# Another layout for the state recurrence of a Mamba block: 16 states x 8 channels on the partitions

## The chip, the core and the metric

The kernel runs on one core of a Trainium2 chip. The metric is the device time of one execution in microseconds; all times below are microseconds unless marked ns. The engines are called PE (matrix engine; PEld its weight loads), DVE (vector engine), ACT (scalar engine), POOL (GpSimd) and SP, whose queue issues the DMAs.

## The reference

Input `x` has 64 channels, 256 steps of t and 128 of f. Layer 0 runs a two-way Mamba block along t and then along f; layer 1 is a windowed two-way convolutional LSTM. The change concerns the recurrence of layer 0, which runs for each of four parameter sets (two passes, two directions):

```python
xz = einsum('nld,ed->nle', rmsnorm(u), in_proj_w); x, z = split(xz, 2)   # 128 channels each
x  = silu(conv1d_depthwise(x, 4 taps) + conv_b)
dt, Bm, Cm = split(x @ x_proj_w.T, [4, 20])                              # 4, 16 and 16 wide
dt = softplus(dt @ dt_proj_w.T + dt_proj_b)                              # 128 channels
A  = -exp(A_log)                                                         # (128, 16)
def step(h, inp):                                                        # h: (n, 128, 16)
    dA = exp(dt_t[:, :, None] * A)
    h = dA * h + dt_t[:, :, None] * B_t[:, None, :] * x_t[:, :, None]
    return (h, einsum('nds,ns->nd', h, C_t))
y = (ys + x * Dp) * silu(z); out = y @ out_proj_w.T + u
```

So for each token there are 128 channels x 16 states: a decay, an input, a recurrence along the sequence, a product with C, and a sum over the states.

## The kernel before, in words

Layer 0 works in two passes, the class `Stage`: along t (stage 0, sequences of 256 tokens) and along f (stage 1, sequences of 128). A chunk is 512 tokens of whole sequences; each pass has 64 chunks. `run` issues, for every chunk: `scan` of direction 0, then `head` of the next chunk (both directions), `scan` of direction 1, and `tail`. The program is written in a framework whose scheduler places each engine's instructions in a fixed order when the program is built and adds the semaphores. A tile pool has a number of buffers for each tag; a new tile waits until the oldest one of its tag is free.

`head` loads `u` (by SP along t, by a POOL copy from `X` along f), normalises it (`sq`, `pm`, `rs`, `unp`), and takes both directions up to the scan's inputs: `px` and `pz` on PE, `xs` and `zs` (Silu) on ACT, `pv` on PE; then softplus over ACT (`e`, `r`, `lw`) and POOL (`w`, `e`, `lw`, `dt`), and `dtx` = dt * x on POOL. B and C (32 rows, `pb`) are split into three bfloat16 parts, stacked in the tile `bc` (L287 to L290), so that a bfloat16 matmul can spread one row over all partitions exactly.

In `scan` the 128 channels lie on the partitions, and the 512 tokens on the free axis. A round g treats two of the 16 states, side by side in 1024 columns; here it is called a pair, and a direction has eight. A pair is, with its lines:

- PE, L315: four bfloat16 matmuls spread B's and C's rows of the two states into PSUM, `bb` and `cc`, one buffer each.
- ACT, L321: two exponentials, dA = exp(A * dt), into one of two fixed buffers per direction.
- DVE, L325: bx = bb * dtx; L327: the scan h = dA * h + bx along 1024 columns; L335: h = h * cc.
- PE, L308: two float32 matmuls with the identity add the states of the pair before to `y`.

At the end of a direction L339 forms `yz` = y * silu(z). `tail` (L348 to L370) multiplies by the output weights, adds the residuals `u`, and ACT puts the result into `X`. A float32 matmul shows as two passes in the profile. Layer 1 follows (lines from L389 on) and is not touched; of its lines, the prediction names L466 (additions of weights on DVE and POOL), L458 (loads of those weights), L577 (matmuls over half of the rows), L605, L612 and L613 (DVE steps on `n` and `v`), and L616 (stores of `y` to `out`).

Of the kernel before, what the change touches and what calls it, by code (L numbers as in the profile page):

```python
"""TF-Mamba block followed by the windowed bidirectional conv-LSTM, on one core.

Layer 0 keeps channels (d = 128) on the partitions and tokens on the free axis.  A chunk is 512
tokens of whole sequences; its two directions share the normalised input.  Products of weights
alone are formed once on the chip: the depthwise taps with in_proj, dt_proj with x_proj, out_proj
with the closing linear layer.  The state recurrence is a scan along the free axis, run backwards
for the flipped direction; a zero decay at a sequence's first token starts it anew.

Layer 1 keeps (parity of f, channel) on the partitions, so that the stride 2 of the windows is a
step of one column.  Taps of the window and of the conv that meet the same column are summed once;  # L10
the four columns at the borders, where the conv's padding drops taps, have their own weights.
"""
# [18 lines left out]
P = 128  # L31
# [4 lines left out]
NBC = 2 * NS  # L36
RANK = 4
# [14 lines left out]
class Mamba:  # L52
    """What the chip keeps of the four parameter sets and the two closing linear layers."""

    def __init__(self, ctx, tc, d):
# [7 lines left out]
        # sel[32 k + s, s, :] = 1 for k = 0, 2, 3: spreads row s of a 32-row block over all  # L63
        # partitions and adds the three blocks.
        self.sel = cp.tile([P, NBC, P], BF16, name="sel")
        nc.vector.memset(self.sel, 0.0)
        for k in (0, 2, 3):
            rows = slice(NBC * k, NBC * (k + 1))
            nc.vector.tensor_copy(
                self.sel[rows],  # L70
                self.ident[rows, rows].unsqueeze(2).to_broadcast([NBC, NBC, P]),
            )

# [20 lines left out]
        # A = -exp(A_log)  # L94
        nc.scalar.preload_act_table_set(EXP_AND_LN)
        self.A = cp.tile([P, 4, NS], F32, name="A")
# [4 lines left out]
        self.G1, self.G2, self.Wz, self.Wdt, self.Wbc, self.Dd, self.W2 = ([] for _ in range(7))  # L101
        self.W3, self.lin_b = [], []
        with tc.tile_pool(name="m_prep", bufs=2) as pp, tc.tile_pool(
# [3 lines left out]
            for i, n in enumerate(("tlin", "flin")):  # L107
# [6 lines left out]
                # Both blocks' residuals and the layer's own: u @ (I + W_f + W_b).  # L114
# [7 lines left out]
            for i in range(4):  # L122
# [17 lines left out]
                # Rows 64-127 of the moving operand lag one token behind rows 0-63.  # L140
# [13 lines left out]
                # B and C, three times; nothing in rows 32-63.  # L154
                wbc = cp.tile([P, 4, NBC], F32, name=f"wbc{i}", tag=f"wbc{i}")
                nc.vector.memset(wbc, 0.0)
                for k in (0, 2, 3):
                    nc.vector.tensor_copy(wbc[:, k], xbc)
                self.Wbc.append(wbc.rearrange("p k s -> p (k s)"))
# [12 lines left out]
class Stage:  # L172
    """One bidirectional pass over all tokens, chunk after chunk: along t, or along f."""

    def __init__(self, ctx, m, stage, L, X):
# [6 lines left out]
        self.io = ctx.enter_context(tc.tile_pool(name=n + "io", bufs=2))  # L182
        self.wk = ctx.enter_context(tc.tile_pool(name=n + "wk", bufs=2))
        self.st = ctx.enter_context(tc.tile_pool(name=n + "st", bufs=2))
        fixed = ctx.enter_context(tc.tile_pool(name=n + "fixed", bufs=1))
        self.ps_mm = ctx.enter_context(tc.tile_pool(name=n + "mm", bufs=3, space=PSUM))
        self.ps_bc = ctx.enter_context(tc.tile_pool(name=n + "bc", bufs=1, space=PSUM))
        self.ps_y = ctx.enter_context(tc.tile_pool(name=n + "y", bufs=1, space=PSUM))

        # The padding columns of unp and the decays that start a sequence stay zero throughout.  # L190
# [17 lines left out]
    def head(self, ch, src):  # L208
        """Loads chunk ch, normalises it, and takes both directions up to the scan's inputs."""
        nc, m, L, nseq = self.nc, self.m, self.L, self.nseq  # L210
        unp = self.unp[ch % 2]
        if self.time:
            u = self.io.tile([C, nseq, L], F32, name="u", tag="u", bufs=3)
            nc.sync.dma_start(out=u, in_=src[:, ch * nseq : (ch + 1) * nseq, :])
            blocks = [(slice(0, C), slice(0, nseq), u, m.ones_lo[0:C])]
        else:
            u = self.io.tile([P, nseq // 2, L], F32, name="u", tag="u", bufs=3)
            rows = slice(ch * nseq // 2, (ch + 1) * nseq // 2)
            nc.gpsimd.tensor_copy(u, self.X[:, rows, :])  # L219
            blocks = [  # L220
                (slice(0, C), slice(0, nseq // 2), u, m.ones_lo),
                (slice(C, P), slice(nseq // 2, nseq), u, m.ones_hi),
            ]

        sq = self.io.tile(list(u.shape), F32, name="sq", tag="sq")
        nc.gpsimd.tensor_mul(sq, u, u)  # L226
# [3 lines left out]
        # (mean + eps) ** -0.5  # L230
# [8 lines left out]
        for d in range(2):  # L239
# [5 lines left out]
            xs = self.wk.tile([P, NTOK], F32, name="xs", tag=f"xs{d}")  # L245
# [3 lines left out]
            zs = self.wk.tile([P, NTOK], F32, name="zs", tag=f"zs{d}")  # L249
# [3 lines left out]
        # One table set serves all functions from here to the next chunk's Silu.  # L253
        with self.tc.issue_after(silu.ins):
            preload = nc.scalar.preload_act_table_set(EXP_AND_LN)
        for d in range(2):
            i = 2 * self.stage + d
            xs, zs = out[d]
            # softplus(v) = max(v, 0) + log(1 + e), e = exp(-|v|); w = fl(1 + e) and
            # log(1 + e) = log(w) + (e - (w - 1)).  # L260
# [3 lines left out]
            r = self.wk.tile([P, NTOK], F32, name="r", tag="r", bufs=1)  # L264
            lw = self.wk.tile([P, NTOK], F32, name="lw", tag="lw", bufs=1)
            w1 = self.wk.tile([P, NTOK], F32, name="w1", tag="w1", bufs=1)
            with self.tc.issue_after(preload.ins):
                nc.scalar.activation(e, pv, AF.Abs, bias=m.dtb[:, i : i + 1])
            nc.scalar.activation(r, pv, AF.Relu, bias=m.dtb[:, i : i + 1])
            nc.scalar.activation(e, e, AF.Exp, scale=-1.0)  # L270
            nc.scalar.activation(lw, e, AF.Ln, bias=1.0)  # L271
            nc.gpsimd.tensor_scalar(w1, e, 1.0, -1.0, ALU.add, ALU.add)  # L272
            nc.gpsimd.tensor_sub(e, e, w1)  # L273
            nc.gpsimd.tensor_add(lw, lw, e)  # L274
            dt = self.wk.tile([P, NTOK], F32, name="dt", tag=f"dt{d}")
            nc.gpsimd.tensor_add(dt, lw, r)  # L276
            dtx = self.wk.tile([P, NTOK], F32, name="dtx", tag=f"dtx{d}")
            nc.gpsimd.tensor_mul(dtx, dt, xs)  # L278
            # B and C without loss as a sum of three bfloat16: rows 0-31 hold the leading 8 bits of
            # the 24, rows 64-95 the next, rows 96-127 the rest. One pass of the tensor engine then  # L280
            # spreads a row over all partitions, and its float32 sum is the float32 it came from.
            lo, mid = slice(3 * NBC, P), slice(2 * NBC, P)
            pb = self.ps_mm.tile([P, NTOK], F32, name="pb", tag="mm")
            nc.tensor.matmul(pb, lhsT=m.Wbc[i], rhs=xs, start=True, stop=True)
            bc = self.wk.tile([P, NTOK], BF16, name="bc", tag=f"bc{d}")
            rest = self.wk.tile([P, NTOK], F32, name="rest", tag="rest", bufs=1)
            nc.scalar.copy(bc, pb)  # L287
            nc.vector.tensor_sub(rest[mid], pb[mid], bc[mid])  # L288
            nc.gpsimd.tensor_copy(bc[mid], rest[mid])
            nc.gpsimd.tensor_sub(bc[lo], rest[lo], bc[lo])  # L290
            out[d] = (xs, zs, dt, dtx, bc)
        return u, out

    def scan(self, d, ins):
        """The state recurrence of one direction and its gated output."""
        nc, m, L = self.nc, self.m, self.L
        i = 2 * self.stage + d
        xs, zs, dt, dtx, bc = ins
        y = self.ps_y.tile([P, NTOK], F32, name="y", tag="y")
        nc.tensor.matmul(y, lhsT=m.Dd[i], rhs=xs, start=True, stop=False)  # L300
        step = slice(None) if d == 0 else slice(None, None, -1)
        live = slice(1, L) if d == 0 else slice(0, L - 1)
        pending = None

        def add_up(g, h):
            for j in range(2):
                last = g == NS // 2 - 1 and j == 1
                nc.tensor.matmul(y, lhsT=m.ident, rhs=h[:, j], start=False, stop=last)  # L308

        for g in range(NS // 2):  # L310
            bb = self.ps_bc.tile([P, 2, NTOK], F32, name="bb", tag="bb")
            cc = self.ps_bc.tile([P, 2, NTOK], F32, name="cc", tag="cc")
            for k, to in ((0, bb), (NS, cc)):
                for j in range(2):
                    nc.tensor.matmul(to[:, j], lhsT=m.sel[:, k + 2 * g + j], rhs=bc, start=True, stop=True)  # L315
            if pending is not None:
                add_up(*pending)
            dA = self.dA[d][g % 2]
            for j in range(2):
                s = 2 * g + j  # L320
                nc.scalar.activation(  # L321
                    dA[:, j, :, live], self.seqs(dt)[:, :, live], AF.Exp, scale=m.A[:, i, s : s + 1]
                )
            bx = self.st.tile([P, 2, NTOK], F32, name="bx", tag="bx")
            nc.vector.tensor_mul(bx, bb, dtx.unsqueeze(1).to_broadcast([P, 2, NTOK]))  # L325
            h = self.st.tile([P, 2, NTOK], F32, name="h", tag="h", bufs=3)
# [8 lines left out]
            nc.vector.tensor_mul(h, h, cc)  # L335
            pending = (g, h)
# [5 lines left out]
    def tail(self, ch, u, yz):  # L342
        """Closing linear layer with the residuals; the result goes to its place in X."""
# [33 lines left out]
    def run(self, src):  # L377
        nch = T * F // NTOK
        u, ins = self.head(0, src)
        for ch in range(nch):  # L380
            yz = [self.scan(0, ins[0])]
            # The next chunk's head fills the gaps of this one's recurrence.
# [4 lines left out]


def group_norm(tc, X, xn, d):  # L389
    """xn = (X - mean) / sqrt(var + eps) * g + b over everything."""  # L390
    nc = tc.nc
    N = float(C * T * F)
    per = T * F * C // P
# [309 lines left out]
```

## Time and profile before

| what | value |
|---|---|
| median of 3 runs (lowest, highest) | 12018.28 (12006.94, 12019.82) |
| span of the profiled execution, first to last instruction | 12017.3 |
| mean granted PE clock | 0.946 |
| pass along t, 60 to 5365 | 5305, 82.9 a chunk |
| pass along f, 5365 to 10833 | 5468, 85.4 a chunk |
| layer 1, 10833 to 12017 | 1184 |
| L327, L335, L325 on DVE, 2048 each, mean | 2345 ns, 1211 ns, 1205 ns |
| L321 on ACT, 4096, mean | 712 ns |
| ACT table loads in layer 0, each | 1283 ns |
| bytes moved by DMA in the whole span | 28.01 MB |

The page gives the profiled execution's span; its time outside that span is not listed, and the span lies within the three runs. A group's line reads: line, engine, operation, written tile <- read tiles, shapes, count | busy time in total, mean ns of one | idle time of the engine before them, and what ended most of it. In an order of time the columns are start, duration, engine, line, operation, tiles, count.

### The profile page before, as it was taken

What the parts mean: (1) busy time and instruction counts of PE and PEld (TensorE: products, weight loads), DVE (VectorE), ACT (ScalarE), POOL (GpSimd) and SP (SyncE); (2) the same over time, 40 slices, a digit from 0 to 9 for tenths busy, and PEclk for the clock granted to TensorE, in tenths of its full rate; (3) what the DMA queues carried; (4) which work ended last, traced back from release to release, by engine and by line L of the source; (5) the groups of instructions that cost most, each with busy time, mean ns of one, the idle gap of its engine ahead of it and who ended that gap; (6) DMA issues with size and microseconds to landing.
All of it is one profiled execution on the core that took longest, in us unless ns stands there. A gap on an engine that the chain in (4) does not pass through costs nothing. (4 is left out here: it accounts for less than half of the span.)

```text
span 12017.3 us, 70162 instructions
## 1 busy us (share of the span) xinstructions
PE 9284.9 (77%) x24028; PEld 3706.5 (31%) x24028; DVE 10185.2 (85%) x7361; ACT 4977.8 (41%) x7263; POOL 3404.9 (28%) x2079
## 2 busy tenths in 40 slices
PE   6777777777777777777777777777777777777999
PEld 2222222222222222222222322223222222223554
DVE  8999999999999999988999999989999999992121
ACT  4444444444444444434444444444444444431111
POOL 3223232232232322323223323233333233221111
PEclk9999999999999999989999999999999999998999
DMA  0000000000000000000000000000000000000000
GB/s 6 2 2 2 2 2 2 2 2 2 2 2 2 2 2 2 2 1 0 0 0 0 0 0 0 0 0 0 0 0 0 0 0 0 0 0 22 8 8 10
DMA packets 15447, 28.01 MB, mean 2 GB/s; under 512 B 4561, under 2 KB 5233, under 8 KB 15089
## 3 DMA queue, kind: packets, MB, share of 16 engines
q1 hardware_dynamic: 15088, 23.53, 0.6%
q8 instruction: 188, 3.08, 0.1%
q14 instruction: 171, 1.39, 0.0%
HBM read 15.14 MB, written 8.39 MB: 2 GB/s over the span
## 5 line engine op out<-in xcount | busy, mean ns | idle before, releaser
L327 DVE TENSOR_TENSOR_SCAN h<-dA,bx 128x1024 f32<-128x1024 f32 x2048 | 4803.2, 2345 | 48.1 <-ACT dA L321 2.0
L321 ACT ACTIVATE dA<-dt,A 128x510 f32<-128x510 f32 (+1 forms) x4096 | 2716.0, 712 | 4846.6 <-DVE h L327 4702.5
L308 PE MATMUL y<-h,ident 128*128 128x512 f32 x8192 | 4186.0, 636 | 197.5 <-DVE h L335 195.1
L335 DVE TENSOR_TENSOR h<-h,cc 128x1024 f32<-128x1024 f32 x2048 | 2479.2, 1211 | 201.1 <-PE cc L315 151.3
L325 DVE TENSOR_TENSOR bx<-bb,dtx 128x1024 f32<-128x1024 f32 x2048 | 2467.2, 1205 | 140.3 <-PE bb L315 131.5
L315 PE MATMUL bb<-bc,sel 128*128 128x512 bf16 x4096 | 1287.6, 396 | 1299.0 <-DVE bx L325 1288.0
L315 PEld LDWEIGHTS <-sel 128*128 128x128 bf16 x8192 | 793.7, 100 | 4618.3 <-issue 4238.6
L308 PEld LDWEIGHTS y<-h,ident 128*128 128x128 f32 x8192 | 1642.9, 203 | 1774.7 <-issue 1139.3
L315 PE MATMUL cc<-bc,sel 128*128 128x512 bf16 x4096 | 1291.7, 398 | 904.3 <-DVE h L335 891.3
L272 POOL TENSOR_SCALAR w<-e 128x512 f32<-128x512 f32 x256 | 596.6, 2331 | 3083.7 <-ACT e L270 3078.0
L553 PE MATMUL pg<-xn,acc 128*128 128x456 f32 x2048 | 815.9, 550 | 0.7 <-ACT gxe L480 0.7
L226 POOL TENSOR_TENSOR sq<-u 64x512 f32<-64x512 f32 (+1 forms) x128 | 179.5, 1403 | 1993.2 <-DMA u<-in_x 1986.3
L612 DVE TENSOR_SCALAR n<-v,slope 128x512 f32<-128x512 f32 x64 | 31.1, 487 | 775.9 <-ACT v L610 774.8
L219 POOL COPY u<-X 128x256 f32<-128x256 f32 x64 | 46.4, 725 | 2144.7 <-PE po L360 2144.6
L276 POOL TENSOR_TENSOR dt<-lw,r 128x512 f32<-128x512 f32 x256 | 515.2, 2013 | 20.1
L553 PEld LDWEIGHTS pg<-xn,acc 128*128 128x128 f32 x2048 | 375.5, 188 | 372.1 <-issue 348.8
L290 POOL TENSOR_TENSOR bc<-rest,bc 32x512 bf16<-32x512 f32 x256 | 452.5, 1767 | 20.4
L288 DVE TENSOR_TENSOR rest<-pb,bc 64x512 f32<-64x512 f32 x256 | 177.7, 694 | 329.5 <-POOL bc L290 177.2
L274 POOL TENSOR_TENSOR lw<-lw,e 128x512 f32<-128x512 f32 x256 | 440.4, 1720 | 20.2
L273 POOL TENSOR_TENSOR e<-e,w 128x512 f32<-128x512 f32 x256 | 402.0, 1570 | 26.2 <-ACT lw L271 6.6
L610 ACT ACTIVATE v<-pproj,bpr 128x512 f32<-128x512 f32 x32 | 22.0, 687 | 774.2 <-PE pproj L605 774.2
L278 POOL TENSOR_TENSOR dtx<-dt,xs 128x512 f32<-128x512 f32 x256 | 335.7, 1311 | 20.2
(129 smaller groups left out, 6911.3 us busy)
## 6 DMA issues: line engine op xcount, KB each, us to landing
u<-in_x SPq DMA_DIRECT2D x64, 128.0 KB, 2.5
out<-y SPq DMA_DIRECT2D x32, 256.0 KB, 2.0
w<-in_W_ih_f SPq DMA_DIRECT2D x5, 512.0 KB, 5.8
w<-in_W_ih_b SPq DMA_DIRECT2D x5, 512.0 KB
cw<-in_conv_w SPq DMA_DIRECT2D x4, 128.0 KB, 3.2
win<-in_in_proj SPq DMA_DIRECT2D x4, 64.0 KB, 2.2
wpr<-in_W_proj SPq DMA_DIRECT2D x1, 256.0 KB, 2.9
ow<-in_out_proj SPq DMA_DIRECT2D x4, 32.0 KB, 1.9
```

What stands on the lines that cost most here:

```text
L272: nc.gpsimd.tensor_scalar(w1, e, 1.0, -1.0, ALU.add, ALU.add)
L273: nc.gpsimd.tensor_sub(e, e, w1)
L274: nc.gpsimd.tensor_add(lw, lw, e)
L276: nc.gpsimd.tensor_add(dt, lw, r)
L290: nc.gpsimd.tensor_sub(bc[lo], rest[lo], bc[lo])
L308: nc.tensor.matmul(y, lhsT=m.ident, rhs=h[:, j], start=False, stop=last)
L315: nc.tensor.matmul(to[:, j], lhsT=m.sel[:, k + 2 * g + j], rhs=bc, start=True, stop=True)
L321: nc.scalar.activation(dA[:, j, :, live], self.seqs(dt)[:, :, live], AF.Exp, scale=m.A[:, i, s : s + 1])
L325: nc.vector.tensor_mul(bx, bb, dtx.unsqueeze(1).to_broadcast([P, 2, NTOK]))
L327: nc.vector.tensor_tensor_scan(h.rearrange("p j n -> p (j n)")[:, step], dA.rearrange("p j n l -> p (j n l)")[:, step], bx.rearrange("p j ...
L335: nc.vector.tensor_mul(h, h, cc)
L553: nc.tensor.matmul(pg[:, :, 2 : 2 + inner], lhsT=acc[:, q, gate * P : (gate + 1) * P], rhs=xv[:, rows, half, q : q + inner], start=q == 0, ...
```

## The change

The tile of the recurrence is turned: the partitions now hold 16 states x 8 channels (partition 8 s + d), and a group is 8 of the 128 channels; there are 16 groups, numbered 4 r + k. A pair is now two groups, (r, k) and (r + 1, k), again 1024 columns.

- `dt` has to be on all 16 states' partitions. It is written to a DRAM tile `there` (256 KB) and read back four times with a repeated source into the tiles `rep` (1 MB each, four buffers of one tag shared by both directions).
- `dtx` is spread by float32 matmuls whose contracted rows are 32 of the partitions (`sel`), into `bx` in PSUM (two buffers). DVE multiplies `bx` by B in place, and the scan reads it from PSUM.
- B and C come out of one float32 matmul each, already repeated over the 8 channels (`Wb`, `Wc`), and are copied to SBUF by ACT; the bfloat16 split is gone.
- The product with C moves from DVE to POOL.
- The sum over the states is a float32 matmul with 32 output columns (`fold`) into 32 of y's partitions, two per pair, in place of the identity matmuls. The input product and the fold are called spread and fold below.
- `sq` moves from POOL to ACT; w = 1 + e and w - 1 move to ACT as two Identity steps, `lw` is Ln of w.
- Pools: `io` 2 -> 1 buffers (`u` 3 -> 2), `wk` 2 -> 3 with tags shared by the directions, `st` 2 -> 3 (so `h` has three, as before).

```diff
+        mask = cp.tile([P, NK, DL], F32, name="mask")
...
+        self.sel = cp.tile([P, NK, P], F32, name="sel")
+        for k in range(NK):
             nc.vector.tensor_copy(
+                self.sel[:, k].rearrange("p (s d) -> p s d", s=NS),
+                mask[:, k].unsqueeze(1).to_broadcast([P, NS, DL]),
             )
+        self.fold = cp.tile([P, NK, 32], F32, name="fold")
...
-        self.io = ctx.enter_context(tc.tile_pool(name=n + "io", bufs=2))
-        self.wk = ctx.enter_context(tc.tile_pool(name=n + "wk", bufs=2))
-        self.st = ctx.enter_context(tc.tile_pool(name=n + "st", bufs=2))
+        self.io = ctx.enter_context(tc.tile_pool(name=n + "io", bufs=1))
+        self.wk = ctx.enter_context(tc.tile_pool(name=n + "wk", bufs=3))
+        self.st = ctx.enter_context(tc.tile_pool(name=n + "st", bufs=3))
+        self.dram = ctx.enter_context(tc.tile_pool(name=n + "dram", bufs=3, space=bass.MemoryType.DRAM))
...
-        self.ps_bc = ctx.enter_context(tc.tile_pool(name=n + "bc", bufs=1, space=PSUM))
+        self.ps_bx = ctx.enter_context(tc.tile_pool(name=n + "bx", bufs=2, space=PSUM))
...
-        nc.gpsimd.tensor_mul(sq, u, u)
+        nc.scalar.activation(sq, u, AF.Square)
...
-            nc.scalar.activation(lw, e, AF.Ln, bias=1.0)
-            nc.gpsimd.tensor_scalar(w1, e, 1.0, -1.0, ALU.add, ALU.add)
-            nc.gpsimd.tensor_sub(e, e, w1)
+            nc.scalar.activation(w, e, AF.Identity, bias=1.0)
+            nc.scalar.activation(lw, w, AF.Ln)
+            nc.scalar.activation(w, w, AF.Identity, bias=-1.0)
+            nc.gpsimd.tensor_sub(e, e, w)
             nc.gpsimd.tensor_add(lw, lw, e)
+            nc.gpsimd.tensor_add(dt, lw, dt)
+            there = self.dram.tile([DL, NG, NTOK], F32, name="there", tag="there")
+            nc.sync.dma_start(out=there.rearrange("d g t -> g d t"), in_=dt)
+            rep = []
+            for r in range(4):
+                t = self.wk.tile([P, NK, NTOK], F32, name="rep", tag="rep", bufs=4)
+                nc.sync.dma_start(
+                    out=t,
+                    in_=there[:, NK * r : NK * (r + 1)].unsqueeze(0).to_broadcast([NS, DL, NK, NTOK]),
+                )
+                rep.append(t)
...
-            nc.scalar.copy(bc, pb)
-            nc.vector.tensor_sub(rest[mid], pb[mid], bc[mid])
-            nc.gpsimd.tensor_copy(bc[mid], rest[mid])
-            nc.gpsimd.tensor_sub(bc[lo], rest[lo], bc[lo])
+            for h, wt in ((0, m.Wb[i]), (1, m.Wc[i])):
+                pb = self.ps_mm.tile([P, NTOK], F32, name="pb", tag="mm")
+                nc.tensor.matmul(pb, lhsT=wt, rhs=xs, start=True, stop=True)
+                t = self.wk.tile([P, NTOK], F32, name="bc", tag=f"bc{h}")
+                nc.scalar.copy(t, pb)
...
+        pairs = [[(r, k), (r + 1, k)] for r in (0, 2) for k in range(NK)]
+        def add_up(n, h):
+            for j, (r, k) in enumerate(pairs[n]):
+                nc.tensor.matmul(
+                    y[32 * r : 32 * r + 32],
+                    lhsT=m.fold[:, k],
+                    rhs=h[:, j],
...
+        for n, pair in enumerate(pairs):
+            bx = self.ps_bx.tile([P, 2, NTOK], F32, name="bx", tag="bx")
+            for j, (r, k) in enumerate(pair):
+                rows = slice(32 * r, 32 * r + 32)
+                nc.tensor.matmul(bx[:, j], lhsT=m.sel[rows, k], rhs=dtx[rows], start=True, stop=True)
             if pending is not None:
                 add_up(*pending)
+            dA = self.dA[d][n % 2]
+            for j, (r, k) in enumerate(pair):
+                g = NK * r + k
                 nc.scalar.activation(
+                    dA[:, j, :, live], self.seqs(rep[r][:, k])[:, :, live], AF.Exp, scale=m.A[:, i, g : g + 1]
                 )
-            bx = self.st.tile([P, 2, NTOK], F32, name="bx", tag="bx")
-            nc.vector.tensor_mul(bx, bb, dtx.unsqueeze(1).to_broadcast([P, 2, NTOK]))
-            h = self.st.tile([P, 2, NTOK], F32, name="h", tag="h", bufs=3)
+            nc.vector.tensor_mul(bx, bx, B.unsqueeze(1).to_broadcast([P, 2, NTOK]))
+            h = self.st.tile([P, 2, NTOK], F32, name="h", tag="h")
             nc.vector.tensor_tensor_scan(
...
-            nc.vector.tensor_mul(h, h, cc)
-            pending = (g, h)
+            nc.gpsimd.tensor_mul(h, h, Cm.unsqueeze(1).to_broadcast([P, 2, NTOK]))
+            pending = (n, h)
```

## The prediction

> **What bounds the kernel now.** I read four views: the engines' totals with the stretches by pass, the groups, the order of time within one chunk, and the few rows that stand for what the change adds. Times are microseconds; a "pair" is one round of the scan loop (two of 16 states), a chunk has 16 pairs, eight per direction.
>
> First the totals, then busy time in the pass along t and the pass along f (columns: stretch, its length, busy time of PE, weight loads, DVE, ACT, POOL, granted clock):
>
> ```profile
> PE 9284.9 (77%) x24028; PEld 3706.5 (31%) x24028; DVE 10185.2 (85%) x7361; ACT 4977.8 (41%) x7263; POOL 3404.9 (28%) x2079
> ...
> 60.00:5365.00 5305.00, 4035.71 (x10206) 1524.72 (x10204) 4895.25 (x3450) 2317.94 (x3432) 1461.39 (x949) 0.95 0.01 2
> 5365.00:10833.00 5468.00, 4109.69 (x10493) 1613.95 (x10493) 5027.21 (x3586) 2486.48 (x3576) 1794.42 (x1030) 0.93 0.00 0
> ```
>
> DVE is busy 92% of both passes. With 64 chunks each, a chunk takes 82.9 along t and 85.4 along f, 84.2 on average. The other 1244 of the span 12017.3 hold start-up and the second layer, which the change leaves alone. The groups say what fills DVE:
>
> ```profile
> L327 DVE TENSOR_TENSOR_SCAN h<-dA,bx 128x1024 f32<-128x1024 f32 x2048 | 4803.2, 2345 | 48.1 <-ACT dA L321 2.0
> L335 DVE TENSOR_TENSOR h<-h,cc 128x1024 f32<-128x1024 f32 x2048 | 2479.2, 1211 | 201.1 <-PE cc L315 151.3
> L325 DVE TENSOR_TENSOR bx<-bb,dtx 128x1024 f32<-128x1024 f32 x2048 | 2467.2, 1205 | 140.3 <-PE bb L315 131.5
> ```
>
> One steady pair in order of time (start, duration):
>
> ```profile
> 5012.26 1.19 DVE L325 TENSOR_TENSOR bx<-bb,dtx 128x1024 f32<-128x1024 f32 x1
> 5013.38 1.20 DVE L335 TENSOR_TENSOR h<-h,cc 128x1024 f32<-128x1024 f32 x1
> 5014.51 2.28 DVE L327 TENSOR_TENSOR_SCAN h<-dA,bx 128x1024 f32<-128x1024 f32 x1
> 5015.06 1.88 PE L308 MATMUL y<-h,ident 128*128 128x512 f32 x4
> 5016.71 1.19 DVE L325 TENSOR_TENSOR bx<-bb,dtx 128x1024 f32<-128x1024 f32 x1
> ```
>
> A pair takes 4.45, back to back on DVE. A float32 matmul of 512 columns is two passes, 0.43 apart: (1.88 - 0.59) / 3.
>
> **Rows for what is added.** POOL beside DVE, POOL's cost of a 1024-wide two-operand step, matmuls on half of the rows, and transfers:
>
> ```profile
> 5004.82 2.28 DVE L327 TENSOR_TENSOR_SCAN h<-dA,bx 128x1024 f32<-128x1024 f32 x1
> 5005.02 3.15 POOL L276 TENSOR_TENSOR dt<-lw,r 128x512 f32<-128x512 f32 x1
> 5007.02 1.20 DVE L325 TENSOR_TENSOR bx<-bb,dtx 128x1024 f32<-128x1024 f32 x1
> 5008.93 1.27 POOL L278 TENSOR_TENSOR dtx<-dt,xs 128x512 f32<-128x512 f32 x1
> ```
> ```profile
> L466 POOL TENSOR_TENSOR hi<-hi,w 128x1024 f32<-128x1024 f32 x8 | 19.7, 2464 | 25.2 <-issue 17.3 <-DMA w<-in_W_ih_f 7.5
> ```
> ```profile
> 11615.19 1.93 PE L577 MATMUL pg<-hs,whh 64*128 64x488 f32 x8
> ```
> ```profile
> out<-y SPq DMA_DIRECT2D x32, 256.0 KB, 2.0
> w<-in_W_ih_f SPq DMA_DIRECT2D x5, 512.0 KB, 5.8
> ```
>
> **DVE, removed.** The C product (16 x 1.21 a chunk), `rest` (2 x 0.69), and the fights of scan and POOL. The third group shows these: L276 stood still while the scan (both operands in SBUF) ran to 5007.05, then finished in 1.1 beside L325, whose one operand is in PSUM. After the change bx is in PSUM, so scan and product each read one operand from SBUF; I price no fights. The Trainium skill ("SBUF — State Buffer", "Who interferes with whom") says the same and extends it to any DVE step with one SBUF input; the scan with one operand in PSUM is in no row here. What remains: product, then a scan that needs it at once. L613 follows L612, which it needs, 0.03 after its end, so 1.20 + 0.03 + 2.28 = 3.5 a pair. Reading and writing bx in PSUM lies between nothing and the 0.02 by which the L325 and L335 rows differ from their minima; I take nothing. Floor of a chunk: 16 x 3.5 = 56.0, two `yz` (0.67), `unp` (2 x 0.67 along t, 4 x 0.42 along f): 58.7 and 59.0.
>
> **POOL.** It loses `w`, two `bc` steps and `sq`, and gains the C product, 2.36 (the uncontended L466; mean 2.46). Per chunk 16 x 2.36 = 37.8 plus eight 512-wide steps of 1.27 = 48: not the bound, but now inside the chain.
>
> **PE.** The four bf16 selections (0.21 apart) go; two spreads (32 rows) and two folds (32 columns), all float32, come. L577 runs eight 64-row passes in 1.93 where eight in a row need 0.57 + 7 x 0.41 = 3.4: passes on different rows overlap. So a pair of spreads, or of folds, costs between 0.86 (overlapped) and 1.72 (L308, not). No row shows different columns; I take 0.86 for both, as L577 is the nearer form, and keep 1.72 for the range. A change of form costs: L349, L351, L300 in the tail start 1.0 apart instead of 0.86, so I take 0.95 for a fold, 1.1 for a spread to its last result. By the Trainium skill ("TensorEngine Tiling (Array Packing)", Key Properties) a change of mode drains the array; a drain is at most the 0.16 between duration and spacing, twice a loop, which would make the sum about 100 more.
>
> **The new chain.** DVE no longer waits only for itself. In the order of the built program PE issues the fold of pair p before the last spread of pair p+2 for ten pairs of a chunk along t and eleven along f; for the others the distance is three, and once a chunk along t it is one. So scan p, 0.1 hand-over, C product 2.36, fold 0.95, spread 1.1, 0.1, product and scan 3.5: 8.1 for two pairs, where DVE alone needs 7.0. I walked one chunk of each pass with these numbers, each queue in its built order; time beyond the floor:
>
> - Along t: the tail's matmuls ahead of the first fold +1.4; distance two +2.8 in all (POOL's backlog covers the rest); at the change of direction fold 7, `pb`, `yz`, the D product, `pb`, then spread 8 stand in a row, 10.9 instead of 4.2, +6.7; `e`, `lw`, `dt`, `dtx` of the next chunk (5.1 on POOL) between C products 8 and 9, then four more, +3.9. Sum 14.8, chunk 73.5.
> - Along f: the same start +1.4; distance two +2.2; seven float32 matmuls of the next chunk and the D product between fold 7 and the second spread of pair 9, +5.5; fold 8 split by `pb`, then `pv` waiting for ACT, +2.7; exps and C products behind the head's steps +5.2. Sum 17.0, chunk 76.0.
>
> **ACT** gains Square, two Identity steps and a copy per direction (about 0.6 each, rows L270, L287): 4 a chunk, and saves some of the 633 table loads of 1.28. Nearly all of the 41 a chunk lies beside DVE; what does not is in the walk. **DMA:** per direction a 256 KB write and four 1 MB reads on SP. The write has a row, 2.0. In the window of L458's loads the rate holds about 410 GB/s, so 1 MB takes 2.0 + 2.6, and 8.5 MB a chunk needs 21 of 75. Bounds: 2.6 to 10 per MB (128 KB in 2.5 is the poorest row). A read waits for `dt` on POOL and for ACT to free one of four `rep` buffers; the next scan's first exp stands in ACT's queue ahead of this scan's exps 13 to 15. In the walk the buffer's data lands 52 to 61 into the chunk, before DVE needs those exps, so nothing; if reads took 10 per MB, ACT would stand 5 to 8 a chunk. Behind these reads on SP is only the `u` load, a chunk early. The first chunk has no cover: +10 once.
>
> Sum: 64 x 73.5 + 64 x 76.0 = 9568, + 1244 + 10 = 10822 against the span of 12017.3; the runs' median 12018.28 is 1 above that span. Forecast 10820.
>
> **Rivals.**
> - *Main case, 50%*: POOL's and PE's chain sets the pace. Its own range, chunk +-3: 10400 to 11250.
> - *Folds on different columns don't overlap, 17%*: each fold +0.86 in about six links of a chunk and PE nearly full, chunk 81: 11600. For: no row shows it. Against: L577.
> - *The chain is covered, 17%*: if the hand-overs are shorter and queues run ahead, the floor of 58.9 plus POOL's block of 5: chunk 64, 9450. Against: POOL's work is placed by order, not by need.
> - *POOL and DVE still fight, 12%, slower*: the 512-wide POOL rows take 1720 and 2013 on average (L274, L276) where 1272 is their undisturbed time, a factor of 1.35 to 1.6. At 1.5 the C product takes 3.5 and head steps 1.9: +6 in the loops, +4 in the block, +5 in scans of 2.6: chunk 90, 12770. It decides once a C product takes over about 3.0, as 16 x 0.6 uses up the 9.4 that a chunk gains. Against: L276 ran beside L325.
> - *The reads starve ACT, 3%, slower*: all 16 engines fetch the same 64 KB. Below 101 GB/s (8.5 MB in 84.2) it is the bound: 12100 and up.
> - *No change, 1%.*
>
> Faster takes the first three, 83% after a share that ends near no change; slower 15%, same 2%. 0.2% (24) is about what a measurement of this kernel can tell from no change. The range leaves out the lower half of the covered case and most of the two slower ones: 9600 to 12000.
>
> **What would show it.** Right: DVE 75 to 82% busy in the passes, scan 2.28 without the long ones, POOL C product near 2.4, DVE's products waiting for PE `bx`, PE's folds waiting for POOL `h`, `rep` landing in 4 to 6. Wrong: folds at 0.43 steps one after the other; C products over 3; ACT waiting for DMA `rep`; DVE over 90% busy.

## The result and the profile after

The changed kernel took 13468.74 us (median of 4 runs, 13467.00 to 13474.46) against 12016.88 for the kernel before (4 runs): ratio 1.1211, 95% interval 1.1195 to 1.1227. It is slower by 12%; the forecast was 10820 (9600 to 12000). In the line numbers after, the spread is L346, the fold L333, the product with B L355, the scan L357, the C product L365, the exponentials L352.

The totals and the granted PE clock by slices of the span, from the page:

```profile
PE 12621.1 (94%) x24548; PEld 3069.7 (23%) x24548; DVE 7933.1 (59%) x5053; ACT 5104.7 (38%) x7921; POOL 6275.9 (47%) x3231
...
PEclk6666666656666666666666666666666666667999
```

The stretches of the pass along t, of the pass along f and of the rest (stretch, its length, busy time of PE, weight loads, DVE, ACT, POOL, granted clock, DMA share, GB/s):

```profile
60.00:6153.00 6093.00, 5790.03 (x10450) 1208.20 (x10449) 3721.83 (x2298) 2377.65 (x3751) 3051.59 (x1529) 0.61 0.43 95
6153.00:12284.00 6131.00, 5685.16 (x10750) 1289.58 (x10750) 3955.24 (x2433) 2548.41 (x3906) 3078.25 (x1606) 0.64 0.42 93
12284.00:13466.00 1182.00, 1112.69 (x3282) 557.52 (x3282) 237.04 (x252) 157.99 (x233) 130.27 (x75) 0.97 0.03 12
```

A chunk takes 95.2 along t and 95.8 along f (before: 82.9 and 85.4); the rest is as before. DVE fell from 92% busy to 61% and 65%. PE rose to 95% and 93%, and the clock it was granted fell from 0.95 and 0.93 to 0.61 and 0.64. The groups:

```profile
L346 PE MATMUL bx<-dtx,sel 32*128 32x512 f32 x8192 | 4969.1, 1007 | 215.0 <-DVE h L357 205.5 <-POOL dtx L307 9.5
L365 POOL TENSOR_TENSOR h<-h,bc 128x1024 f32<-128x1024 f32 x2048 | 4843.4, 2365 | 5743.0 <-DVE h L357 5724.9 <-PE y L333 11.9 <-PE bx L346 4.5
L357 DVE TENSOR_TENSOR_SCAN h<-dA,bx 128x1024 f32<-128x1024 f32 x2048 | 4681.5, 2286 | 275.2 <-ACT dA L352 41.5 <-DVE bx L355 5.7
L333 PE MATMUL y<-h,fold 128*32 128x512 f32 x8192 | 3639.6, 969 | 468.6 <-POOL h L365 468.6
L352 ACT ACTIVATE dA<-rep,A 128x510 f32<-128x510 f32 (+1 forms) x4096 | 2731.2, 712 | 3722.3 <-DVE h L357 3112.4 <-DMA rep<-there 604.7
L355 DVE TENSOR_TENSOR bx<-bx,bc 128x1024 f32<-128x1024 f32 x2048 | 2505.1, 1223 | 3590.2 <-PE bx L346 3588.2
```

DVE's product waits 3588 for the spread. POOL's C product waits 5725 for DVE, and PE's fold waits only 469 for POOL. So the wait ends at PE, which itself hardly waits: PE is the bound. Two steady pairs in order of time show why:

```profile
3004.46 1.92 PE L333 MATMUL y<-h,fold 128*32 128x512 f32 x4
3005.36 1.21 DVE L355 TENSOR_TENSOR bx<-bx,bc 128x1024 f32<-128x1024 f32 x1
...
3005.58 2.36 POOL L365 TENSOR_TENSOR h<-h,bc 128x1024 f32<-128x1024 f32 x1 [1.18 <-DVE h L357]
...
3006.31 2.08 PE L346 MATMUL bx<-dtx,sel 32*128 32x512 f32 x4
3006.70 2.29 DVE L357 TENSOR_TENSOR_SCAN h<-dA,bx 128x1024 f32<-128x1024 f32 x1
...
3008.32 1.92 PE L333 MATMUL y<-h,fold 128*32 128x512 f32 x4
3008.90 1.21 DVE L355 TENSOR_TENSOR bx<-bx,bc 128x1024 f32<-128x1024 f32 x1
```

From fold to fold PE needs 3.86 (1.85 to the spread's start, 2.01 back to the next fold), while DVE's work of a pair is 3.5. The single records behind these rows say what a row of four passes is: two passes, on different rows or columns, start 6 ns apart, and the next two follow 0.85 later in a fold and 1.01 later in a spread. At full clock, which the same kernel has for some stretches of each chunk, they follow 0.45 and 0.53 later, and from the last pass of one kind to the first of the other it is 0.52: a fold then costs 0.98 and a spread 1.06, against the prediction's 0.95 and 1.1. The clock records know only 0.5 and 1.0, and in 69% of the recorded time it was 0.5. A spread whose partner stands elsewhere in PE's order costs as much as two side by side: 1.05 at full clock, 2.00 at half.

### The profile page after: what moved, and what is told of

Same layout as the page of the kernel before. It is cut to its first block, busy times and chain, and to the rows that moved or that the text cites. A ratio compares the mean times of both kernels' runs of the same rounds, so it can differ in the third digit from the quotient of the medians.

```text
span 13466.5 us, 75072 instructions
## 1 busy us (share of the span) xinstructions
PE 12621.1 (94%) x24548; PEld 3069.7 (23%) x24548; DVE 7933.1 (59%) x5053; ACT 5104.7 (38%) x7921; POOL 6275.9 (47%) x3231
## 5 line engine op out<-in xcount | busy, mean ns | idle before, releaser
L365 POOL TENSOR_TENSOR h<-h,bc 128x1024 f32<-128x1024 f32 x2048 | 4843.4, 2365 | 5743.0 <-DVE h L357 5724.9
L346 PE MATMUL bx<-dtx,sel 32*128 32x512 f32 x8192 | 4969.1, 1007 | 215.0 <-DVE h L357 205.5
L357 DVE TENSOR_TENSOR_SCAN h<-dA,bx 128x1024 f32<-128x1024 f32 x2048 | 4681.5, 2286 | 275.2 <-ACT dA L352 41.5
L355 DVE TENSOR_TENSOR bx<-bx,bc 128x1024 f32<-128x1024 f32 x2048 | 2505.1, 1223 | 3590.2 <-PE bx L346 3588.2
L352 ACT ACTIVATE dA<-rep,A 128x510 f32<-128x510 f32 (+1 forms) x4096 | 2731.2, 712 | 3722.3 <-DVE h L357 3112.4
L333 PE MATMUL y<-h,fold 128*32 128x512 f32 x8192 | 3639.6, 969 | 468.6 <-POOL h L365 468.6
L346 PEld LDWEIGHTS bx<-dtx,sel 32*128 32x128 f32 x8192 | 1233.6, 275 | 3973.9 <-issue 3518.4
L333 PEld LDWEIGHTS y<-h,fold 128*32 128x32 f32 x8192 | 376.6, 134 | 3208.9 <-POOL h L365 2325.5
L311 PE MATMUL pb<-xs,wbc 128*128 128x512 f32 x1024 | 530.7, 628 | 0.0
L261 PE MATMUL px<-unp,g 128*128 128x512 f32 x512 | 469.4, 1015 | 59.0 <-DVE unp L254 59.0
L262 PE MATMUL px<-unp,g 128*128 128x512 f32 x512 | 403.3, 880 | 0.0
L324 PE MATMUL y<-xs,dd 128*128 128x512 f32 x512 | 365.9, 802 | 0.0
```

The costliest lines, as they stand in the source:

```text
L261: nc.tensor.matmul(self.seqs(px), lhsT=m.G1[i], rhs=unp[:, :, first : first + L], start=True, stop=False)
L262: nc.tensor.matmul(self.seqs(px), lhsT=m.G2[i], rhs=unp[:, :, second : second + L], start=False, stop=True)
L311: nc.tensor.matmul(pb, lhsT=wt, rhs=xs, start=True, stop=True)
L333: nc.tensor.matmul(y[32 * r : 32 * r + 32], lhsT=m.fold[:, k], rhs=h[:, j], start=False, stop=n % NK == NK - 1, skip_group_check=True,)
L346: nc.tensor.matmul(bx[:, j], lhsT=m.sel[rows, k], rhs=dtx[rows], start=True, stop=True)
L352: nc.scalar.activation(dA[:, j, :, live], self.seqs(rep[r][:, k])[:, :, live], AF.Exp, scale=m.A[:, i, g : g + 1])
```

## The experiments

Times without an interval are of one run; kernels before on the same chips took 12011 to 12017. "Clock" is the mean granted clock of the whole span.

**Which matmuls lower the clock: all rows, all columns, both.** The order of PE's instructions in the first of these is the changed kernel's, instruction for instruction. In the other two the scheduler placed them differently: 264 spreads stand alone between folds or other matmuls, in the changed kernel 1205.

```diff
 # spread: all 128 rows, weights zero outside the group's 8 channels
-matmul(bx[:, j], lhsT=m.sel[rows, k], rhs=dtx[rows])
+matmul(bx[:, j], lhsT=m.sel[:, NK * r + k], rhs=dtx)
 # fold: all 128 columns, weights zero outside the group's 8 columns
-matmul(y[32 * r : 32 * r + 32], lhsT=m.fold[:, k], rhs=h[:, j])
+matmul(y, lhsT=m.fold[:, P - DL - DL * g : 2 * P - DL - DL * g], rhs=h[:, j])     # g = NK * r + k
```

> The spread of dtx as one matmul over all 128 rows (selection weights padded with zeros) in place of 32 rows; folds stay at 32 columns. After the change PE was busy 95% of the passes at a granted clock of 0.61; two passes on different rows or columns start 6 ns apart, but a pass takes 0.85 us instead of 0.43. Theory A, the clock gate gives half the clock where the matmuls use only a part of the array: here half of the passes use the whole array, the clock rises to 0.8 or more, a spread costs 0.86 in place of 0.5 and the time falls although PE's work at equal clock grows from 2.0 to 2.7 us a pair: 10,900 to 12,200. Theory B, the clock does not follow the shape of the matmuls (it answers to the gaps between them, or to something else), so more PE work at clock 0.6 only costs: 2 x 1.7 + 1.9 = 5.3 us a pair in place of 3.9, time 15,500 to 16,500.

> The fold as a matmul over all 128 columns (weights padded with zeros, added into all of y) in place of 32 columns; spreads stay at 32 rows. Theory A (half clock where only a part of the array is used): clock 0.8 or more, 10,900 to 12,200, like the spread over all rows. If the gate counts rows alone, the fold used all 128 rows before as well, so this run stays at clock 0.6 and 15,500 and the run with the full spread does not. If it counts columns alone, it is the other way round. Theory B: both 15,500 to 16,500.

> Spread over all rows and fold over all columns: no matmul of the scan loop uses a part of the array. PE's work at full clock is 3.44 us a pair, 55 in the loops and about 15 in the head and tail, 70 a chunk. Theory A: granted clock 0.9 to 0.95 as in the kernel before, the chain scan, C product, fold, spread, product, scan 9.5 for two pairs: chunk 80 to 87, time 11,500 to 12,400. Theory B: clock 0.6, 6.9 us a pair and 110 and more in the loops, time over 17,000.

Measured: all rows 11675 (clock 0.964), all columns 14069 (0.824), both 13046 (0.965). The page's clock by slices of the first and of the second, and the first one's groups on PE:

```profile
PEclk9999999999999999999999999999999999999999
```
```profile
PEclk8888888888888888887887778887878788787999
```
```profile
L340 PE MATMUL bx<-dtx,sel 128*128 128x512 f32 x8192 | 4288.1, 636 | 331.6 <-DVE h L351 295.0 <-POOL dtx L302 9.5 <-PE y L328 0.3
...
L328 PE MATMUL y<-h,fold 128*32 128x512 f32 x8192 | 2327.8, 632 | 1336.4 <-POOL h L359 1336.0
```

A spread that does twice the work made the kernel 1793 us faster. The fold, which was not touched, went from 969 to 632 ns in the mean. So the clock is what was lost, and the spread's 32 rows lose it: theory B is out. Columns are not rows: with the fold over all columns the clock came back only in part, although each pair gave PE as much more to do as in the first run. Of theory A's expectation for that run the clock came (0.8 or more), the time (10,900 to 12,200) did not. The third run shows the price of giving up the fold's overlap at full clock: 13046 - 11675 = 1371, with the other order of PE in it. The expectation of 11,500 to 12,400 for it missed: the fold stands inside the chain through POOL, and 1371 / 2048 = 0.67 a pair showed in the time of the 0.86 that each pair's folds cost more.

**Is it POOL's place in the chain instead?**

```diff
-nc.gpsimd.tensor_mul(h, h, Cm...)
+nc.vector.tensor_mul(h, h, Cm...)
```

> Only the C product goes back from POOL to DVE. If PE at half clock sets the pace (3.86 us a pair, back to back, 95% busy), a DVE with 4.7 us a pair has 16 x 4.7 + 3 = 79 us of work in a chunk of 95, PE keeps its work, and the time changes little: 12,900 to 13,500, clock still near 0.6. If POOL's 2.36 us step in the chain is what costs, the time falls to DVE's 79 to 85 a chunk: 11,400 to 12,200.

Measured: 12626, clock 0.701. This missed both windows. PE stayed near half clock, 90% busy, so the clock is still what is short; but the time fell by 842, more than "little". With the C product off POOL, PE's folds waited 351 instead of 469 and more of the time had the full clock (40% instead of 31%); PE's order changed too (636 spreads alone instead of 1205). The causes are not apart in this run; the last experiment below has the C product on DVE at full clock.

**Extra work that only raises the activity, and a fixed order.** Two things were changed at once here: matmuls of ones were added, and the order was fixed so that the fold of pair n - 1 stands directly behind the spreads of pair n. One of the three runs has that order alone.

```diff
+for j in range(2):                       # only in the runs with extra work; 0:32 columns in the second
+    matmul(bx[:, j], lhsT=ones_bf16[:, 0:128], rhs=ones_bf16)
 for j, (r, k) in enumerate(pair):        # issued behind the last fold
     matmul(bx[:, j], lhsT=m.sel[rows, k], rhs=dtx[rows])
 if pending: add_up(*pending)             # issued behind both spreads
```

> The changed kernel with its 32-row spreads and 32-column folds, each pair's two spreads and two folds kept next to each other on PE, and two bf16 matmuls of ones (128 rows x 128 columns x 512) put into each bx ahead of the spreads, which overwrite them: pure extra work of 2 x 0.21 us a pair at full clock. Theory rows (from the clock records of the six traces so far: a stretch of 3.41 us is granted the full clock if in the stretch before the matmuls' time, weighed by the share of the 128 rows that they use, was over about 0.38 of the stretch at full clock; the loop of the changed kernel has 0.37): the loop now has about (0.86 + 0.43 + 0.43) / 3.6 = 0.48, the clock is 0.93 or more and the time 10,500 to 11,300, where the prediction's sum without the clock's fall stands. Theory B (the clock follows something else): 0.6, PE 4.7 us a pair, time 13,500 to 15,000.

> The same with matmuls of ones that use all 128 rows but only 32 columns. Theory rows: the columns in use do not count, so the loop has 0.48 as with 128 columns; clock 0.93 or more, time within 2% of the run with 128 columns. Theory rows times columns: the loop has (0.43 + 0.43 + 0.11) / 3.6 = 0.27, less than in the kernel before or in the run with full spread and fold, whose limit by this measure is 0.38: clock 0.55 to 0.7, time 13,000 to 14,500.

> The changed kernel with nothing added; only the order on PE is fixed, so that the two spreads of a pair and the two folds of a pair stand next to each other (in the changed kernel about 1200 of the 4096 spreads stand alone, and cost a full 2.0 us at half clock each instead of half of that). Theory rows: the loop keeps 0.37 or less, so the clock stays at 0.5 to 0.65; PE saves about 600 x 2.0 us = 1200 at half clock: 11,800 to 12,900. Theory that the interleaving itself makes the clock fall: 0.9 or more and 10,500 to 11,200.

Measured: extra work over 128 columns 14604 (clock 0.786), over 32 columns 14707 (0.768), order alone 14242 (0.688). All three missed; what held is that the first two lie within 2% of each other, and the first one's time (not its clock) lies in theory B's window. The order alone was 773 slower than the changed kernel. The line of waits (total, times, longest) that goes with it is

```profile
PE y L334 <- POOL h L369: 2936.2, 1230, 5.7
```

In the changed kernel the fold waited 469 for POOL's C product, here 2936: the next spread stands behind a fold whose C product is not finished, so C product, fold, spread, product and scan follow each other for every two pairs. In the changed kernel's order five of a chunk's 16 folds stand one pair further back, and most of the others have the first spread of the next pair ahead of them; here none has. Further down one pair more is given, and the time falls well below the changed kernel's. What the extra work does tell: 128 or 32 columns differ by 0.7%, so the columns in use count for little.

**The spread in bfloat16.** dtx is split into a high and a low part, and two bf16 matmuls over all rows take the place of the float32 one.

```diff
+nc.scalar.copy(split[:, 0], dtx); nc.vector.tensor_sub(split[:, 1], dtx, split[:, 0])
-matmul(bx[:, j], lhsT=m.sel[rows, k], rhs=dtx[rows], start=True, stop=True)
+matmul(bx[:, j], lhsT=sel_bf16[:, NK * r + k], rhs=split[:, 0], start=True, stop=False)
+matmul(bx[:, j], lhsT=sel_bf16[:, NK * r + k], rhs=split[:, 1], start=False, stop=True)
```

> The spread as two bf16 matmuls of 128 rows (dtx split into a high and a low bf16 part, two steps more per direction on ACT and DVE) instead of one float32 matmul of 32 rows: 4 x 0.21 = 0.86 us a pair with all rows in use. Theory rows: the loop has (0.86 + 0.86) / 3.55 = 0.48: clock 0.93 or more. Compared with the float32 spread over all rows (11,675) PE saves 0.86 a pair: time 10,700 to 11,300. Theory B: 0.6 and over 12,500.

Measured: 12304, clock 0.802: both windows missed. All rows are in use, and the clock is still not full. PE now has so little to do that its waits for POOL (1509 at the fold) leave much of the time empty. So rows alone are not enough; that rows times time counts is argued below.

**One pair more between C product and fold, with and without all rows.** The fold of pair n - 2 now stands behind the spreads of pair n. The two runs without extra work have the same order of PE's instructions, instruction for instruction; the one with 32 rows has four h buffers, the one with all rows three.

```diff
-pending = (n, h)                          # fold of pair n - 1 behind the spreads of pair n
+pending.append((n, h))                    # fold of pair n - 2 behind the spreads of pair n
```

> 32-row spreads and 32-column folds as in the changed kernel, but the order on PE is fixed so that the fold of pair p stands behind the spreads of pair p+2 (distance three, where the run with adjacent pairs had two and lost 770 us by it), both spreads and both folds of a pair next to each other, with a fourth h buffer. Nothing is added. Theory rows: at DVE's floor of 3.54 a pair the loop has (0.86 + 0.43) / 3.54 = 0.36, at the limit of 0.34 to 0.38 that the ten traces show; a late start drops it below: clock 0.6 to 0.8, PE 3.86 a pair in the half-clock stretches, time 11,000 to 12,800. If the clock follows the order alone: 0.9 and 10,300.

> The same order, and one bf16 matmul of ones (128 rows x 128 columns x 512, 0.21 us at full clock) put into each pair's bx ahead of the spreads, which overwrite it: extra work only. Theory rows: (0.86 + 0.43 + 0.21) / 3.6 = 0.42: clock 0.9 or more, loops near DVE's 3.54 a pair, time 9,900 to 10,900, and so less than without the dummy by 1000 or more. Theory B (clock follows something else than the rows in use): not faster than without it, 11,500 to 13,500.

> The float32 spread over all 128 rows with the same order (three h buffers). Theory rows: (0.86 + 1.72) / 3.54 = 0.73, clock 0.95 or more; PE 16 x 3.0 + 16 = 64 a chunk against DVE's 59: 10,000 to 11,000, against 11,675 in the changed kernel's own order. If the order does not matter at full clock: 11,500 to 11,800.

Measured: 32 rows 12119 (clock 0.704), 32 rows and extra work 12665 (0.766), all rows 10796 (0.973). The first is 2123 faster than the run with spreads and folds kept together and one pair less between C product and fold (14242). The passes of the first and of the third:

```profile
60.00:5497.00 5437.00, 4996.04 (x10452) 1076.53 (x10451) 3782.95 (x2298) 2556.59 (x3875) 3031.67 (x1530) 0.66 0.47 107
5497.00:10935.00 5438.00, 4962.25 (x10750) 1144.77 (x10750) 3836.03 (x2433) 2538.77 (x3906) 3068.03 (x1606) 0.69 0.47 105
```
```profile
60.00:4849.00 4789.00, 4239.45 (x10447) 1242.09 (x10445) 3748.36 (x2298) 2537.29 (x3874) 3052.57 (x1529) 0.96 0.53 121
4849.00:9612.00 4763.00, 4218.90 (x10750) 1276.61 (x10750) 3843.88 (x2433) 2529.19 (x3906) 3076.91 (x1606) 0.99 0.53 120
```

With the same order, chunks of 85.0 and 85.0 become 74.8 and 74.4. PE is busy 757 and 743 less although it does more. Some steady pairs of the third run:

```profile
4035.06 1.05 PE L329 MATMUL y<-h,fold 128*32 128x512 f32 x4
4035.84 1.21 DVE L353 TENSOR_TENSOR bx<-bx,bc 128x1024 f32<-128x1024 f32 x1
...
4036.07 2.35 POOL L363 TENSOR_TENSOR h<-h,bc 128x1024 f32<-128x1024 f32 x1 [4.82 <-DVE h L355]
4036.07 1.96 PE L343 MATMUL bx<-dtx,sel 128*128 128x512 f32 x4
...
4037.18 2.29 DVE L355 TENSOR_TENSOR_SCAN h<-dA,bx 128x1024 f32<-128x1024 f32 x1
...
4038.47 1.05 PE L329 MATMUL y<-h,fold 128*32 128x512 f32 x4 [0.44 <-POOL h L363]
```

Fold 1.05 and spread 1.96 lie inside DVE's 3.5. The extra work failed for the second time, and the window that came is the one of theory B. Its order of PE also differs from the run without it (1272 spreads alone instead of 512). Along f it lifted the clock from 0.69 to 0.82, with chunks of 84.1 instead of 85.0; along t it did not (0.68, chunks of 94.4).

What follows was worked out afterwards, from the records. The clock changes only after multiples of 3.41 us. For every such stretch I added up the matmuls' time at full clock, weighed by the rows they use out of 128 (passes side by side on different columns once), as a share of the stretch. Over the 16 traces, a share over 0.37 is followed by a full-clock stretch and one below it by a half-clock stretch in 97% of the cases (least 89% in one trace). Time without the weight sorts 90%, rows times columns 92%, columns 76% (87% if passes side by side on different rows count once), each at its best limit.

With this the changed kernel's loop reads as follows. If DVE set the pace at full clock, the share would be (0.86 + 0.43) / 3.54 = 0.36, at the limit at best; this is an estimate, as the trace has no such stretch. Its full-clock stretches with spreads and folds alone are 64 in which PE works off a backlog (share 0.51 or more, all followed by full clock) and 72 in which it mostly stands still (0.19 or less, all followed by half clock). At half clock a packed PE shows (1.71 + 0.86) / 3.86 / 2 = 0.33, below the limit, so the loop cannot climb out and waits for the 128-row matmuls of a head or tail. The trace agrees: of 1731 half-clock stretches with spreads and folds alone, one is followed by full clock, and 259 of the 260 rises come after a stretch with a matmul of head or tail in it. One extra bf16 matmul makes the share (1.71 + 0.86 + 0.43) / 4.4 / 2 = 0.34: still below. With all rows a packed PE shows (1.71 + 3.41) / 5.56 / 2 = 0.46 at half clock and climbs out: in the third run 33 of 38 such stretches are followed by full clock, in the first, with the same order, 1 of 1271. This sorting is worked out from records; what the clock's control counts inside is not shown.

**What the rest of the sum was worth at full clock.** The bf16 spread with the later fold, the C product back on DVE with all rows, and the all-rows version timed:

> Spread by two bf16 matmuls over all 128 rows, as in the earlier bf16 run (12,304, clock 0.80), now with the fold of pair p behind the spreads of pair p+2 (three h buffers). Theory rows: at DVE's floor (0.86 + 0.86) / 3.54 = 0.49, over the limit of about 0.37; PE only 16 x 2.0 + 16 = 48 a chunk: clock 0.9 or more and 10,200 to 10,800, a little less than the float32 spread over all rows (10,796), as PE leaves DVE's way. If waits for POOL hold PE below the limit, as in the earlier bf16 run: clock near 0.8, 11,000 to 12,000.

> The run with the float32 spread over all rows and the later fold (10,796, clock 0.97), with the C product on DVE instead of POOL. It tells what moving the C product to POOL is worth at full clock. DVE has 16 x (1.2 + 1.2 + 2.3) + 3 = 79 a chunk instead of 59. Theory that DVE's load was rightly seen as the bound of the kernel before: 11,500 to 11,900. If the chain through POOL costs what DVE saves: 10,600 to 11,000.

> The float32 spread over all 128 rows with the later fold once more, timed in five rounds beside the kernel before: 10,790 to 10,810, a ratio of 0.898 to 0.900.

Measured: bf16 11711 (ratio 0.9745, 0.9728 to 0.9762; clock 0.838): the second window of its expectation, its fold still waiting 1523 for POOL. C product on DVE 11814 (clock 0.985): DVE is 93% busy along t again (4597 of 4940), and having the C product on POOL is worth 11814 - 10796 = 1018 when the clock is full. The all-rows version with the later fold: 10798.07, ratio 0.8986, 95% interval 0.8973 to 0.8998. It beats the kernel before by 10% and the changed one by 20%; it differs from the changed kernel only in the spread's rows and in the order on PE: a later fold, and spreads kept together.

## Why the prediction was wrong

**The step that failed** is the term PE: "I take 0.86 for both", with passes 0.43 apart. That duration comes from rows at a clock of 0.95, and the change itself took that clock away. The overlap and the costs of a change of form were right at full clock (fold 0.98, spread 1.06); the granted clock was carried over from the old matmuls to the new ones. In the half-clock stretches, 69% of the recorded time, a fold measured 1.85 and a spread 2.01. The loop there became PE's 3.86 a pair instead of DVE's 3.5, spreads standing alone (1205 rows of two passes) cost a full 2.0 each, and the head's matmuls ran partly at half clock as well. No rival held this; the nearest, "folds on different columns don't overlap", has the right engine with the wrong mechanism, and its 11600 was too low.

**DVE, removed: right.** The scan took 2286 ns (2345 before), equally with and without a C product on POOL beside it (2286 either way by the records). What the prediction took from the Trainium skill ("SBUF — State Buffer", "Who interferes with whom"; the page excepts the 2-port modes) agrees with these rows: one operand of the scan and of the product lies in PSUM. What the sum passed over is `unp`, which has both operands in SBUF: where it met a C product it waited for its end (along f 2.0 instead of 0.42, two of four a chunk). The prediction's row of L327 ends at 5007.10, not 5007.05; nothing hangs on it.

**POOL: right.** 2365 ns against 2.36, eight steps of 1.27. The rival of a fight is out for scan and C product.

**The chain: right where the clock is full.** With all rows and the changed kernel's order, chunks were 78.3 and 84.7 (5013 and 5419 over 64). The sum's 73.5 and 76.0 plus 0.86 for the wider spread in five links a chunk and in two at the direction's start is 79.5 and 82.0, an estimate made afterwards. An unchanged 32-row loop at full clock could not be had, so 10820 itself stays untested. That the best version lands at 10798 is chance: it has the dearer spread and a better order.

**The order** was seen (fold of pair p before the last spread of p + 2; the trace has it for the ten and eleven pairs named) but priced at 2.8 and 2.2 a chunk. At full clock, all rows, one pair more of distance for these pairs, with the spreads kept together (512 alone instead of 1205), took 11675 to 10796: 879 or 6.9 a chunk, with the same work.

**DMA: twice as dear as summed, and nearly hidden; ACT: right.** A pair of reads (2 MB) took about 10 to move, 210 GB/s against the 410 of the row taken; the first landed 7.2 after its issue and the second 11.3 (medians), against 4.6. This lies inside the bounds of 2.6 to 10 per MB. ACT waited 605 in all for `rep`, the scan only 41.5 for ACT; in the fastest version it was 1280 and 276, so the reads are closer to the pace there.

**Of what would show it**, the rows for POOL and scan came as listed, and DVE's products did wait for PE's `bx`, though for the clock's sake. "DVE 75 to 82% busy" (61 to 65%), "folds waiting for POOL" (469 in all) and "`rep` landing in 4 to 6" (7 to 11) did not come, and the clock was not on the list. The Trainium skill's page "TensorE: Matmul & The Clock Gate" (Part 1) says that activity in windows of about 3.4 us releases the clock. The multiples of 3.41 us in the clock records agree; but a PE that the profile counts as 95% busy was granted 0.61, so busy time as the profile counts it does not decide.

## What to carry to other kernels

When a change replaces full matmuls by ones on a part of the array, first work out what share of time times rows is left in the loop, and price PE at half clock wherever that share comes near what the trace shows as the limit (here 0.37). Zero-padding a matmul to all rows can be the faster form although it does more: here giving up the spreads' overlap cost less than the lost clock (11675 against 13469). Padding the fold's columns, which had not cost the clock, was a loss of 1371. Where a queue holds both the end of a long chain and the start of the next round, issue the end a round later.

## What the runs showed of the hardware

- The clock follows rows far more than columns: 32-row spreads alone 0.82 (fold over all columns), 32-column folds alone 0.96 (spread over all rows).
- The half-clock state holds itself: a loop of 32-row spreads and full-row folds that would be near the limit of 0.37 at full clock shows 0.33 at half clock, and 1 of its 1731 half-clock stretches was followed by full clock. The changed kernel's median chunk was 95.57 in both passes (from the starts of `yz`), 28 stretches of 3.413.
- Overlap needs a neighbour: a 32-row spread alone cost 1.05 at full clock, two side by side 1.06.
- A DVE step with two SBUF operands stands still beside POOL's long steps: `unp` of 64x256 took 1999 ns in the mean, 421 for the one just before it, and the long ones ended 0.28 us after the end of a POOL step.

```profile
L254 DVE TENSOR_TENSOR unp<-u,rs 64x256 f32<-64x256 f32 x128 | 255.9, 1999 | 2.8
...
L253 DVE TENSOR_TENSOR unp<-u,rs 64x256 f32<-64x256 f32 x128 | 53.9, 421 | 33.9 <-ACT rs L251 31.9
```
